# Two attention layers on one core: row position terms from PSUM, one transfer per query block, and half of the division on ScalarE

## The chip, the cores and the metric

The kernel runs on one core of one Trainium2 chip. The metric is the device time in microseconds. A core has a matrix engine (PE, TensorE), a vector engine (DVE, VectorE), an activation engine (ACT, ScalarE), a general engine (POOL, GpSimd) and a sequencer that only issues transfers (SP, SyncE). Each works through its own instructions in order and waits on semaphores. PE writes into PSUM, which DVE and ACT can read; the other data lie in SBUF or in DRAM.

## What is computed

Two layers, each `x = x + attention(group_norm(x))`, on an input of 4 images of 32 x 32 positions (S = 1024) with 768 channels, in float32. There are 12 heads of 64 channels. For one image and one head:

```python
q, k, v  = split(group_norm(x) @ Wqkv)          # layer 1 has biases too
rel_h    = einsum('hwc,hkc->hwk', q, Rh)         # Rh[h,k] = rel_pos_h[h - k + 31]
rel_w    = einsum('hwc,wkc->hwk', q, Rw)         # Rw[w,k] = rel_pos_w[w - k + 31]
scores   = scale * q @ k.T + rel_h[..., :, None] + rel_w[..., None, :]
out      = softmax(scores) @ v
x        = x + concat_heads(out) @ Wproj + bproj
```

The position terms depend on the query and on the key's row (rel_h) or column (rel_w) alone. Layer 1 clips its tables at 14 positions and scales differently; the shape of the work is the same.

## The kernel before

Layers and images are taken one after another: 8 "images" (layer, image), each with 6 pairs of heads, 48 pairs g in all. The two heads of a pair lie in the lower and upper 64 of 128 partitions. A pair is cut into 8 blocks n of 128 queries, four image rows each. The loop over units (g, n) at the end of `attention_blocks` writes the order out by hand. In unit (g, n) it emits, for every engine in this order: what is due in the list `early`; the biases of the unit after next (POOL); the scores of the next unit (PE), with their reduction (DVE) and exponential (ACT); the reads due from `behind`; the transposes of this unit (`turn`, DVE); the division of the next unit (`divide`); then a share of other products from the list `todo`, by `take`; and, after blocks 2 and 6, `weigh`, the product of weights and values. So the tight loop of a unit runs scores, reduction, exponential, reciprocal, division, transpose, write to DRAM, read back, weigh, spread over several units.

The other products are the projections of the next pair (`project_in` for q and k, `project_values` for v) and the output products (`project_out`). They are cut into chunks, and `shares` says how many chunks a unit takes. `later` and `early` are lists of small steps: what is put in `later` in a unit runs at the start of the unit after next or, if a step of `early` puts it there, of the next one.

Position terms: `positions` multiplies a half of q (4 blocks) by both tables, 128 columns a head, of which the first 64 are for the row and the last 64 for the column. ACT copies the whole result from PSUM into t (L286) and sends it to DRAM (tdr, L288). `diagonals` then reads both kinds of terms back with shifted strides into rel, 16 transfers of 32 KB a pair (L307). The row term of a query needs 32 of 63 table entries, and the start of the 32 depends on the image row only, which is the same for 32 neighbouring partitions.

Transposing the weights: `turn` transposes 32 x 32 squares on DVE (L370) into tb. A tile tb holds two blocks of one head; after the second block both heads' tiles are written to DRAM (td, L373), 1 MB each, and queued in `behind` or `behind2`. `read_back` (L381) reads a tile into pt with keys in the partitions. `weigh` (L399) multiplies one or two quarters (two blocks each) by the values of both heads, and DVE evicts the sum (L408 in layer 0, L411 with a bias in layer 1).

Buffers that matter: two PSUM tiles `ps_s` for scores, and two PSUM tiles `ps_m` that projections, position terms, weigh and output products take in turns, so that a product can start only when the product before last has been evicted. The projections are evicted by ACT and then DVE (L227 or L229, then L230; L259, then L260).

Queues: SP issues nearly all transfers in order, and waits in that order. ACT issues tdr; in the first pair it also issues half of rel, and at the very end the last reads of pt.

At the end, the last pair has no projections ahead of it. Its `todo` holds the rest of the last image's output products in three parts (`cuts`): channels 0 to 2, channels 3 and 4, and channel 5, which is the last pair itself. Its first 30 chunks run in the units, 12 after them, then two weighs and the last six products.

Of the kernel before, what the change touches and what calls it, by code (L numbers as in the profile page):

```python
# [31 lines left out]
FP = mybir.dt.float32  # L32
AF = mybir.ActivationFunctionType
ALU = mybir.AluOpType
ENGINES = {getattr(mybir.EngineType, e) for e in ("PE", "DVE", "Activation", "Pool", "SP")}

P = 128
B, HW, C = 4, 32, 768
S = HW * HW
NH, D = 12, 64  # L40
NC = C // P
NT = S // P
# [5 lines left out]
NP = NH // 2  # L48
# [6 lines left out]
def attention_blocks(ctx: ExitStack, tc: tile.TileContext, a: dict, out: bass.AP):  # L55
    nc = tc.nc
# [7 lines left out]
    qkpool = ctx.enter_context(tc.tile_pool(name="qk", bufs=2))  # L64
    vpool = ctx.enter_context(tc.tile_pool(name="v", bufs=3))
    scpool = ctx.enter_context(tc.tile_pool(name="sc", bufs=6))
    tmppool = ctx.enter_context(tc.tile_pool(name="tmp", bufs=1))
    tbpool = ctx.enter_context(tc.tile_pool(name="tb", bufs=3))
    ptpool = ctx.enter_context(tc.tile_pool(name="pt", bufs=2))
    relpool = ctx.enter_context(tc.tile_pool(name="rel", bufs=2))  # L70
    iopool = ctx.enter_context(tc.tile_pool(name="io", bufs=4))
    small = ctx.enter_context(tc.tile_pool(name="small", bufs=4))
    dram = ctx.enter_context(tc.tile_pool(name="scratch", bufs=1, space=bass.MemoryType.DRAM))
    dram2 = ctx.enter_context(tc.tile_pool(name="scratch2", bufs=2, space=bass.MemoryType.DRAM))
    ps_s = ctx.enter_context(tc.tile_pool(name="ps_s", bufs=2, space=PSUM))
    ps_m = ctx.enter_context(tc.tile_pool(name="ps_m", bufs=2, space=PSUM))
# [2 lines left out]
    mid = [dram.tile([C, S], FP, tag=f"mid{b}", name=f"mid{b}") for b in range(B)]  # L79
# [4 lines left out]
    NPAIR = NI * NP  # L84
# [33 lines left out]
    for l in range(LAYERS):  # L118
        tab = const.tile([P, 2, 2 * HW], FP, tag=f"tab{l}", name=f"tab{l}")
        nc.gpsimd.memset(tab, 0.0)  # L120
        for i, ax in enumerate("hw"):
            src = a[f"rel{ax}{l}"]
            n = src.shape[1]
# [10 lines left out]
    for l in range(LAYERS):  # L134
        t = const.tile([P, NC], FP, tag=f"bo{l}", name=f"bo{l}")
        nc.sync.dma_start(out=t, in_=a[f"bo{l}"])
        bo.append(t)
    bqkv = const.tile([P, 3, NP], FP, tag="bqkv", name="bqkv")
# [130 lines left out]
    def positions(g, i):  # L269

        l = images[g // NP][0]
        q = qk_of[g, 0]
        if i == 0:
            t_of[g] = dram2.tile([S, 2 * P], FP, tag="tdr", name=f"tdr_{g}")
            rel_of[g] = relpool.tile([P, 2, 2, NT, HW], FP, tag="rel", name=f"rel_{g}")
        ps = ps_m.tile([P, 2, 4, P], FP, tag="m", name=f"tp_{g}_{i}")
        for j in range(4):
            for h in range(2):
                rows = slice(h * D, (h + 1) * D)
                at = 4 * i + j  # L280
                nc.tensor.matmul(  # L281
                    ps[:, h, j, :], lhsT=q[rows, at * P : (at + 1) * P], rhs=tabs[l][rows, :],
                    start=True, stop=True,
                )
        t = tmppool.tile([P, 4, 2, P], FP, tag="tmp", name=f"t_{g}_{i}")
        nc.scalar.copy(t, ps.rearrange("p h j r -> p j h r"))  # L286
        td = t_of[g]
        nc.scalar.dma_start(  # L288
            out=td[i * HALF : (i + 1) * HALF, :].rearrange("(j p) r -> p j r", p=P),
            in_=t.rearrange("p j h r -> p j (h r)"),  # L290
        )
        if i == 1:
            later.append(lambda: diagonals(g))

    def diagonals(g):
        td = t_of[g]
        for h in range(2):
            for ax in range(2):
                for y in range(4):


                    at = HW * y * 2 * P + h * P + HW - 1 + 2 * HW * ax - (y if ax == 0 else 0)
                    src = bass.AP(
                        td.tensor, td.offset + at,
                        [[2 * P - ax, HW], [P * 2 * P - (4 if ax == 0 else 0), NT], [1, HW]],
                    )
                    (nc.scalar if h and not g else nc.sync).dma_start(out=rel_of[g][32 * y : 32 * y + 32, h, ax, :, :], in_=src)  # L307


    sc_of, st_of, tb_of, pt_of, attn_of = {}, {}, {}, {}, {}  # L310
# [39 lines left out]

    def divide(g, n):
        st = st_of[g, n]
        nc.vector.reciprocal(st[:, 2, :], st[:, 1, :])  # L353
        for h in range(2):
            sc = sc_of[g, n, h].rearrange("p k j -> p (k j)")
            nc.gpsimd.tensor_scalar(sc, sc, st[:, 2, h : h + 1], 1.0, ALU.mult, ALU.mult)  # L356

    def turn(g, n):

        quarter, j = divmod(n, 2)
        for h in range(2):
            if j == 0:
                tb_of[h] = tbpool.tile([P, HW, 2, HW], FP, tag="tb", name=f"tb_{g}_{n}_{h}")
            tb = tb_of[h]
            nc.vector.transpose(tb[:, :, j, :], sc_of[g, n, h])  # L370
            if j == 1:
                td = dram2.tile([P, S * 2], FP, tag=f"td{h}", name=f"td_{g}_{n}_{h}")
                nc.sync.dma_start(out=td, in_=tb.rearrange("p k n i -> p (k n i)"))  # L373
                (behind if quarter % 2 else behind2).append(
                    lambda queue=None, h=h, td=td: read_back(g, quarter, h, td, queue)
                )

    def read_back(g, quarter, h, td, queue=None):
        pt = ptpool.tile([P, 4, NT, 2 * HW], FP, tag=f"pt{h}", name=f"pt_{g}_{quarter}_{h}")
        pt_of[g, quarter, h] = pt  # L380
        (queue or nc.sync).dma_start(  # L381
            out=pt.rearrange("p r k t -> p r (k t)"),
            in_=td.rearrange("(r j) (a t) -> (j a) r t", r=4, a=4),
        )

    def weigh(g, quarters):

        if quarters[0] == 0:
            attn_of[g] = apool.tile([P, S], FP, tag="attn", name=f"attn_{g}")
        n = len(quarters)
        av = ps_m.tile([P, S], FP, tag="m", name=f"av_{g}_{quarters[0]}")[:, : n * 2 * P]
        for at, quarter in enumerate(quarters):
            for k in range(NT):
                for h in range(2):
                    rows = slice(h * D, (h + 1) * D)
                    nc.tensor.matmul(  # L399
                        av[rows, at * 2 * P : (at + 1) * 2 * P], lhsT=v_of[g][:, k, rows],  # L400
                        rhs=pt_of[g, quarter, h][:, :, k, :], start=(k == 0), stop=(k == NT - 1),
                    )
        at = quarters[0] * 2 * P
        to = attn_of[g][:, at : at + n * 2 * P].rearrange("p (q n r i) -> p q r n i", q=n, n=2, r=4)
        av = av.rearrange("p (q r n i) -> p q r n i", q=n, n=2, r=4)
        im, pair = divmod(g, NP)
        if images[im][0] == 0:
            nc.vector.tensor_copy(to, av)  # L408
        else:
            for q in range(n):  # L410
                nc.vector.tensor_scalar(to[:, q], av[:, q], bqkv[:, 2, pair : pair + 1], None, ALU.add)  # L411

    def cuts(im):
        return [0, NC // 2, NC] if im + 1 < NI else [0, NC // 2, NC - 1, NC]
# [86 lines left out]

    early, mid, later, behind, behind2 = [], [], [], [], []

    def run(todo):
        while todo:  # L510
            todo.pop(0)()
# [12 lines left out]
    def take(groups, n):  # L524

        while groups and n > 0:
            group, count = groups[0]
            if next(group, None) is None:
                groups.pop(0)
            else:  # L530
                groups[0] = (group, count - 1)
                n -= 1
        while groups and groups[0][1] == 0:
            for _ in groups.pop(0)[0]:
                pass
# [6 lines left out]
    with tc.manual_schedule(engines=ENGINES):  # L542
# [8 lines left out]
        todo = prepare(0)  # L551
# [14 lines left out]
        for at, (g, n) in enumerate(units):  # L566
            im, pair = divmod(g, NP)
            end = im + 1 == NI
            if n == 0:
                shares = [6, 6, 0, 6, 12, 6, 0, 12]  # L570
                ins = (todo if at == 0 else []) + prepare(g + 1)
                if pair < 3:
                    if at == 0:
                        shares = [12, 6, 0, 6, 12, 6, 0, 0]
                    todo = ins + (put_out(im - 1, 1, range(4 * pair, 4 * pair + 4)) if im else [])
                elif pair < NP - 1:
                    todo = ins + put_out(im, 0, range(4 * pair - 12, 4 * pair - 8))
                    if pair == 3 and not end:
                        stages, apply = norm(im + 1)
                else:  # L580
                    todo = ins + put_out(im, 0, range(8, 12))
                    if end:
                        fetch_last()
                        todo += put_out(im, 1, range(12)) + put_out(im, 2, range(0, 12, 2))
                        shares = [6, 6, 0, 6, 6, 2, 0, 4]
            if (pair, n) in loads and not end:
                load_x(im + 1, loads[pair, n])
            if im + 1 < B:
# [9 lines left out]
                biases(*units[at + 2])  # L598
            if at + 1 < len(units):
                scores(*units[at + 1])  # L600
            run(behind)
            behind, behind2 = behind2, behind
            if pair == 3 and n in stages and not end:
                stages[n]()
            if pair == 4 and n in (2, 4, 6) and not end:
                apply(n // 2 - 1)
            share = shares[n]
            first = 3 if n == NT - 1 else 2 if end and pair == NP - 1 and n in (3, 4) else 0
            first = min(first, share)
            take(todo, first)  # L610
            share -= first
# [11 lines left out]
                weigh(g, (0, 1))  # L623
            elif n == 2 and g:
                weigh(g - 1, (2, 3))
        for read in behind:
            read(nc.scalar)
        take(todo, 12)
        for quarter in (2, 3):
            weigh(NPAIR - 1, (quarter,))  # L630
        todo = put_out(NI - 1, 2, range(1, 12, 2))
# [56 lines left out]
```

## Time and profile before

| | us |
|---|---|
| median of 3 runs (3507.12 to 3509.28) | 3508.29 |
| the profiled execution's span | 3507.0 |
| median less that span | 1.3 |
| PE busy | 3462.3 (99%) |
| POOL busy | 2729.9 (78%) |
| DVE busy | 2381.1 (68%) |
| ACT busy | 1227.5 (35%) |
| weight loads of PE, beside its products | 1921.4 (55%) |
| DMA, mean rate over the span | 309 GB/s |

The profile is of one execution. Busy time is what an engine spent in instructions; a group of instructions is named by line, engine, operation and "written<-read" tiles, with the count and the mean duration. A wait is the idle time of an engine before an instruction, put down to what released it. The chain of waits follows the work that ended last back to the start. Most matrix products work in two halves of PE side by side, so their durations add up to more than PE's busy time. The profile counts two records for one float32 matmul. Granted clock is the share of PE's full clock. Transfers in DRAM and back are named by the tile written and the tile read, and can be followed from issue to landing.

### The profile page before, as it was taken

The numbers are of one execution on the slowest core, as the hardware profiler recorded it, in microseconds if no ns is written. First come the engines' busy times: TensorE is split into PE (matmuls) and PEld (weight loads), VectorE is DVE, ScalarE is ACT, GpSimd is POOL, SyncE is SP. The second block draws the span as 40 slices with busy tenths as digits, with TensorE's granted clock in tenths as the row PEclk, the third lists the DMA queues.
The fourth block names the chain that finished last, engine by engine and source line by source line (L and its number), as shares of the span: only waits on it lengthen the run. The fifth ranks groups of instructions, "written<-read, shape, count | busy, mean of one in ns | idle before, by whom it ended". The sixth has DMA issues, their size and how long they took to land.

```text
span 3507.0 us, 55102 instructions
## 1 busy us (share of the span) xinstructions
PE 3462.3 (99%) x21120; PEld 1921.4 (55%) x21120; DVE 2381.1 (68%) x3676; ACT 1227.5 (35%) x2040; POOL 2729.9 (78%) x1546
## 2 busy tenths in 40 slices
PE   6999999999999999999999999999999999999999
PEld 4555555555555555555555555555555555555554
DVE  4666767767677676767767667666666667666666
ACT  2334333333333333333333333333333333333331
POOL 3888887778777787788777788787787778787774
PEclk9999999999999999999999999999999999999999
DMA  4889989999899898898989989899889988898877
GB/s 137 312 308 311 332 293 337 319 316 326 304 329 323 313 316 313 312 324 305 326 305 326 320 292 332 311 331 306 300 327 324 321 298 316 319 322 295 311 275 281
DMA packets 624857, 1084.54 MB, mean 309 GB/s; under 512 B 247120, under 2 KB 310096, under 8 KB 575440
## 3 DMA queue, kind: packets, MB, share of 16 engines
q1 hardware_dynamic: 569008, 1028.29, 83.4%
q10 hardware_dynamic: 55584, 52.72, 4.4%
q8 instruction: 166, 2.72, 0.3%
q14 instruction: 99, 0.81, 0.1%
HBM read 580.59 MB, written 500.27 MB: 308 GB/s over the span
## 4 chain that ended last, share of the span: by engine, by line
PE 97%; DMA 2%; DVE 0%; SPq 0%; issue 0%; ACT 0%; POOL 0%; ACTq 0%; DVEq 0%
PE pj L214 28%; PE s L333 19%; PE av L399 19%; PE o L475 14%; PE pv L249 14%; PE tp L281 3%; DMA tdr<-t 1%; DMA pt<-td 1%; SPq L307 0%; DMA td<-tb 0%; DMA wo<-in_wo 0%; DMA xn<-in_x 0%; DVE st L152 0%; DMA rel<-tdr 0%; DMA per<-mv 0%
## 5 line engine op out<-in xcount | busy, mean ns | idle before, releaser
L319 POOL TENSOR_TENSOR sc<-rel 128x1024 f32<-128x1024 f32 x768 | 1890.4, 2485 | 38.2 <-DMA rel<-tdr 38.2
L356 POOL TENSOR_SCALAR sc<-sc,sm 128x1024 f32<-128x1024 f32 x768 | 855.1, 1127 | 686.1 <-DVE sm L353 669.2
L346 ACT ACTIVATE sc<-sc,sm 128x1024 f32<-128x1024 f32 x768 | 879.8, 1147 | 1370.9 <-DVE sm L342 1368.7
L342 DVE CUSTOM_DVE_ANT_0 sc<-s,sc 128x1024 f32<-128x1024 f32 x768 | 909.8, 1222 | 293.3 <-PE s L333 266.4
L214 PE MATMUL pj<-xn,w 64*128 64x512 f32 x4608 | 1033.5, 591 | 26.8 <-DVE xn L193 25.7
L370 DVE STREAM_TRANSPOSE tb<-sc 128x1024 f32<-128x1024 f32 x768 | 910.7, 1222 | 22.9 <-DMA td<-tb 20.5
L214 PEld LDWEIGHTS pj<-xn,w 64*128 64x128 f32 x4608 | 453.2, 188 | 568.6 <-issue 536.6
L333 PE MATMUL s<-k,q 64*128 64x512 f32 x3072 | 750.1, 598 | 7.0 <-DVE sm L342 6.9
L399 PE MATMUL av<-pt,v 128*64 128x256 f32 x6144 | 689.1, 382 | 6.1 <-DMA pt<-td 6.1
L399 PEld LDWEIGHTS av<-pt,v 128*64 128x64 f32 x6144 | 434.5, 137 | 289.8 <-ACT v L259 35.6
L249 PE MATMUL pv<-wv,xn 64*128 64x256 f32 x4608 | 515.7, 376 | 0.0
L249 PEld LDWEIGHTS pv<-wv,xn 64*128 64x128 f32 x4608 | 448.3, 187 | 90.8 <-issue 30.1
L475 PE MATMUL o<-attn,wo 128*128 128x512 f32 x1080 | 475.8, 597 | 0.2 <-DMA wo<-in_wo 0.2
L333 PEld LDWEIGHTS s<-k,q 64*128 64x128 f32 x3072 | 288.5, 187 | 299.5 <-issue 275.5
L475 PEld LDWEIGHTS o<-attn,wo 128*128 128x128 f32 x1080 | 201.4, 190 | 271.4 <-issue 260.9
L260 DVE TENSOR_TENSOR v<-pv,v 128x256 f32<-128x256 f32 x192 | 81.5, 425 | 277.6 <-ACT v L259 277.6
L259 ACT COPY v<-pv 128x256 f32<-128x256 f32 x192 | 71.5, 372 | 330.7 <-PE pv L249 282.9
L286 ACT COPY t<-tp 128x1024 f32<-128x1024 f32 x96 | 97.2, 1012 | 245.5 <-PE tp L281 148.5
L346 ACT ACTIVATION_READ_ACCUMULATOR sc<-sc,sm 128x1 f32 x768 | 143.6, 187 | 0.0
L230 DVE TENSOR_TENSOR q<-pj,q 128x512 f32<-128x512 f32 x96 | 66.4, 692 | 107.5 <-ACT q L227 56.0
L230 DVE TENSOR_TENSOR k<-pj,k 128x512 f32<-128x512 f32 x96 | 66.4, 692 | 95.5 <-ACT k L227 49.0
L281 PEld LDWEIGHTS tp<-tab,q 64*128 64x128 f32 x1536 | 100.0, 187 | 39.9 <-issue 39.6
(34 smaller groups left out, 787.6 us busy)
## 6 DMA issues: line engine op xcount, KB each, us to landing
td<-tb SPq DMA_DIRECT2D x384, 1024.0 KB, 5.9
pt<-td SPq DMA_DIRECT2D x382, 1024.0 KB, 7.6
tdr<-t ACTq DMA_DIRECT2D x96, 512.0 KB, 6.3
w<-in_wqk SPq DMA_DIRECT2D x96, 384.0 KB, 7.5
rel<-tdr SPq DMA_DIRECT2D x760, 32.0 KB, 2.3
part<-res SPq DMA_DIRECT2D x84, 256.0 KB, 5.5
res<-part SPq DMA_DIRECT2D x84, 256.0 KB, 9.1
wv<-in_wv SPq DMA_DIRECT2D x24, 768.0 KB, 8.7
```

The costliest lines, as they stand in the source:

```text
L214: nc.tensor.matmul(t[:, a, :], lhsT=w[rows, c, :], rhs=xn[c][rows, cols], start=(c == 0), stop=(c == NC - 1),)
L230: nc.vector.tensor_tensor(to, t[1], to, ALU.add)
L249: nc.tensor.matmul(t[:, a, k, :], lhsT=xn[c][rows, (2 * i + k) * P : (2 * i + k + 1) * P], rhs=w[rows, c, :], start=(c == 0), stop=(c == N ...
L281: nc.tensor.matmul(ps[:, h, j, :], lhsT=q[rows, at * P : (at + 1) * P], rhs=tabs[l][rows, :], start=True, stop=True,)
L319: nc.gpsimd.tensor_tensor(sc.rearrange("p (a k) (u l) -> p a (k u) l", a=4, l=8), rel[:, h, 0, n, :].unsqueeze(1).unsqueeze(3).to_broadcas ...
L333: nc.tensor.matmul(ps[h][:, cols], lhsT=q[rows, n * P : (n + 1) * P], rhs=k[rows, cols], start=True, stop=True,)
L342: nc.vector.tensor_tensor_reduce(out=sc, in0=ps[h], in1=sc, scale=-scale, scalar=BIG, op0=ALU.add, op1=ALU.min, accum_out=st[:, 0, h : h + 1],
L346: nc.scalar.activation(sc, sc, AF.Exp, bias=st[:, 0, h : h + 1], scale=-1.0, accum_out=st[:, 1, h : h + 1],)
L356: nc.gpsimd.tensor_scalar(sc, sc, st[:, 2, h : h + 1], 1.0, ALU.mult, ALU.mult)
L370: nc.vector.transpose(tb[:, :, j, :], sc_of[g, n, h])
L399: nc.tensor.matmul(av[rows, at * 2 * P : (at + 1) * 2 * P], lhsT=v_of[g][:, k, rows], rhs=pt_of[g, quarter, h][:, :, k, :], start=(k == 0) ...
L475: nc.tensor.matmul(t, lhsT=wo_of[im, o, c], rhs=attn_of[im * NP + c][:, cols], start=(c == c0), stop=(c == c1 - 1),)
```

## The change

Six things are changed.

1. Row terms: after the table product, ACT copies only the column half (64 of 128 columns) into t, and sends that to DRAM. Then ACT copies the row terms straight from PSUM into rel, four copies of 32 partitions per half. `diagonals` reads back the column terms alone, 8 transfers a pair. t has two buffers instead of one.
2. A tile tb holds one block of both heads. It is written in one transfer of 1 MB, once per block, and read back in one transfer of 1 MB; pt holds two blocks of both heads. tb has two buffers instead of three, td five instead of two per head. The list `behind` becomes four lists in rotation. The reads fall in the same units as before.
3. The second head is divided by ACT instead of POOL; in the last pair both heads are.
4. The sums of `weigh` are evicted by ACT instead of DVE, in one instruction.
5. In the last pair the units take 18 chunks instead of 30, and 24 instead of 12 follow after the last unit; the last unit takes none ahead of its transposes.
6. The builder reserves 1024 bytes a partition of scratch memory for transfers instead of its default.

```diff
-    tmppool = ctx.enter_context(tc.tile_pool(name="tmp", bufs=1))
-    tbpool = ctx.enter_context(tc.tile_pool(name="tb", bufs=3))
+    tmppool = ctx.enter_context(tc.tile_pool(name="tmp", bufs=2))
+    tbpool = ctx.enter_context(tc.tile_pool(name="tb", bufs=2))
...
+    dram4 = ctx.enter_context(tc.tile_pool(name="scratch4", bufs=5, space=bass.MemoryType.DRAM))
...
-        t = tmppool.tile([P, 4, 2, P], FP, tag="tmp", name=f"t_{g}_{i}")
-        nc.scalar.copy(t, ps.rearrange("p h j r -> p j h r"))
+        t = tmppool.tile([P, 4, 2, 2 * HW], FP, tag="tmp", name=f"t_{g}_{i}")
+        nc.scalar.copy(t, ps[:, :, :, 2 * HW :].rearrange("p h j r -> p j h r"))
...
+        for y in range(4):
+            rows = slice(y * HW, (y + 1) * HW)
+            at = ps[rows, :, 0, HW - 1 - 4 * 4 * i - y : 2 * HW - 1 - 4 * 4 * i - y]
+            src = bass.AP(at.tensor, at.offset, [at.ap[0], at.ap[1], [P - 4, 4], [1, HW]])
+            nc.scalar.copy(rel_of[g][rows, :, 0, 4 * i : 4 * i + 4, :], src)
...
     def diagonals(g):
         td = t_of[g]
         for h in range(2):
-            for ax in range(2):
-                for y in range(4):
...
+            for y in range(4):
+                src = bass.AP(
+                    td.tensor, td.offset + HW * y * P + h * 2 * HW + HW - 1,
+                    [[P - 1, HW], [P * P, NT], [1, HW]],
+                )
+                (nc.scalar if h and not g else nc.sync).dma_start(
+                    out=rel_of[g][y * HW : (y + 1) * HW, h, 1, :, :], in_=src
+                )
...
     def divide(g, n):
         st = st_of[g, n]
+        last = g + 1 == NPAIR
...
-            nc.gpsimd.tensor_scalar(sc, sc, st[:, 2, h : h + 1], 1.0, ALU.mult, ALU.mult)
+            if h == 0 and not last:
+                nc.gpsimd.tensor_scalar(sc, sc, st[:, 2, h : h + 1], 1.0, ALU.mult, ALU.mult)
+            else:
+                nc.scalar.mul(sc, sc, st[:, 2, h : h + 1])
 
     def turn(g, n):
...
+        tb = tbpool.tile([P, HW, 2, HW], FP, tag="tb", name=f"tb_{g}_{n}")
         for h in range(2):
...
+            nc.vector.transpose(tb[:, :, h, :], sc_of[g, n, h])
+        td = dram4.tile([P, S * 2], FP, tag="td", name=f"td_{g}_{n}")
+        nc.sync.dma_start(out=td, in_=tb.rearrange("p k h i -> p (k h i)"))
+        behind[(2, 1, 1, 0)[n % 4]].append(lambda queue=None: read_back(g, n, td, queue))
+
+    def read_back(g, n, td, queue=None):
+        quarter, u = divmod(n, 2)
+        if u == 0:
+            pt_of[g, quarter] = ptpool.tile(
+                [P, 2, 4, NT, 2, HW], FP, tag="pt", name=f"pt_{g}_{quarter}"
+            )
         (queue or nc.sync).dma_start(
-            out=pt.rearrange("p r k t -> p r (k t)"),
+            out=pt_of[g, quarter][:, u].rearrange("p r k h i -> p r (k h i)"),
...
-                        rhs=pt_of[g, quarter, h][:, :, k, :], start=(k == 0), stop=(k == NT - 1),
+                        rhs=pt_of[g, quarter].rearrange("p n r k h i -> p (n r) k h i")[:, :, k, h, :],
+                        start=(k == 0), stop=(k == NT - 1),
...
-            nc.vector.tensor_copy(to, av)
+            nc.scalar.copy(to, av)
         else:
-            for q in range(n):
-                nc.vector.tensor_scalar(to[:, q], av[:, q], bqkv[:, 2, pair : pair + 1], None, ALU.add)
+            nc.scalar.activation(to, av, AF.Identity, bias=bqkv[:, 2, pair : pair + 1])
...
-                        shares = [6, 6, 0, 6, 6, 2, 0, 4]
+                        shares = [3, 3, 0, 3, 3, 2, 0, 4]
...
-            run(behind)
-            behind, behind2 = behind2, behind
+            run(behind[0])
+            behind.append(behind.pop(0))
...
-            first = 3 if n == NT - 1 else 2 if end and pair == NP - 1 and n in (3, 4) else 0
+            first = 0 if at + 1 == len(units) else 3 if n == NT - 1 else 2 if end and pair == NP - 1 and n in (3, 4) else 0
...
-        for read in behind:
-            read(nc.scalar)
-        take(todo, 12)
+        for reads in behind:
+            for read in reads:
+                read(nc.scalar)
+        take(todo, 24)
...
-    nc = bacc.Bacc("TRN2", target_bir_lowering=False, num_devices=1)
+    nc = bacc.Bacc("TRN2", target_bir_lowering=False, num_devices=1, dynamic_dma_scratch_size=1024)
```

## The prediction

> **What bounds the kernel now.** I read the waits of TensorE first, then busy time by stage, then the timeline where a wait stood. The page gives PE 3462.3 us of a span of 3507.0. All that PE waited for, longest first (total us, times, longest):
>
> ```profile
> PE pj L214 <- DVE xn L193: 25.7, 1, 25.7
> PE s L333 <- DVE sm L342: 6.9, 6, 1.4
> PE av L399 <- DMA pt<-td: 6.1, 3, 3.0
> ```
>
> The first is the start, before anything is normalized; the change leaves it. Between 206 and 3410 us there is a single wait, of 1.4 us: the middle is PE end to end. Stages of one pair of heads each, and the last pair (length; busy time of PE, PEld, DVE, ACT, POOL; granted clock; DMA share; GB/s):
>
> ```profile
> 1000.00:1071.69 71.69, 71.69 (x444) 39.80 (x442) 51.97 (x83) 24.93 (x43) 56.59 (x33) 1.00 0.89 317
> 2000.00:2071.69 71.69, 71.69 (x442) 39.81 (x440) 47.95 (x80) 27.98 (x46) 56.50 (x33) 1.00 0.88 313
> 3418.10:3503.90 85.80, 81.64 (x345) 36.49 (x344) 57.01 (x86) 16.64 (x28) 42.41 (x26) 0.98 0.80 284
> ```
>
> A pair takes 71.69 us, all PE; work taken from POOL, DVE or DMA there buys nothing. Time can be won only where PE stood: first pair and last pair. The first pair, chain of work (start, us, what), then PE's timeline:
>
> ```profile
> 92.17 12.20 DMA tdr<-t
> ...
> 113.77 8.84 DMA pt<-td
> ```
> ```profile
> 119.04 0.65 PE L399 MATMUL av<-pt,v 128*64 128x256 f32 x2 [0.74 <-DMA pt<-td]
> 122.66 5.35 PE L399 MATMUL av<-pt,v 128*64 128x256 f32 x30 [2.98 <-DMA pt<-td]
> 127.94 1.99 PE L333 MATMUL s<-k,q 64*128 64x512 f32 x8
> ```
>
> The position transfer tdr landed at 104.4; SP, which issues in order, stood behind it, then issued 16 rel transfers (8.8 us), and only then the reads of pt that weigh needs. The last pair, the chain again:
>
> ```profile
> 3472.64 2.29 DVE tb L370 x2
> 3474.95 6.29 DMA td<-tb
> ...
> 3481.33 10.04 DMA pt<-td
> ```
>
> From the last transpose to the last pt 16.4 us pass in DMA, more than PE had work left to cover.
>
> **What the Trainium skill says.** "TensorE: Matmul & The Clock Gate", Part 1: an idle window of some 3.4 us halves PE's clock. The trace agrees: after the 2.4 us wait near 3491 the granted clock is 0.59, and it is 0.79 at 120 to 125 us. A wait costs more than its length. "ScalarE: Activation LUTs", section on table sets: copies and identities are in every set; the trace agrees, its 16 table loads stand at L181 and L346 alone, so the new multiplies and copies load none. "SBUF — State Buffer", Door 1: runs of at least a 16-byte line read at full rate; weigh's new runs are 128 bytes, and no run here shows it.
>
> **The change, part by part.**
>
> *Position terms.* Per half: the copy t is 512 elements a partition, not 1024: 586 ns (row of L227) for 1012. Four row copies of 256 elements, priced by L259's 372 ns, come behind t's DMA issue. ACT gains 384 x 0.372 - 96 x 0.426 = 102 us. tdr goes from 512 to 256 KB, 96 times; rel reads from 768 to 384, 32 KB each. On SP a pair issues 8 fewer, about 0.5 us each with gaps: 4.4 us.
>
> First pair, start: t's copy ends 0.43 earlier (47.15), the transfer, 2.91 for twice the size, I take as 2.5; 4 issues per queue instead of 8 save 2.1 us of the 4.2 on SP. POOL's first bias starts at 54.0, not 56.73. PE's second scores then wait only for their predecessors' two DVE reductions (1.15 each behind scores ending 59.3): they end near 63.2 instead of 64.4. Gain 1.2 us, at most 2.4 (the two waits), at least 0.
>
> First pair, weigh: with two tmp buffers ACT no longer waits for the first tdr. The second tdr is issued near 89.8, not 92.2: the multiply queued ahead of it holds it to there. Even if it lands as slowly (12.2), SP is free at 102, issues 8 rel in 4.4 us, reads at about 106.5, landing 8.8 later at 115.5; quarter 1 of weigh needs it at about 117. Both waits go. Between the scores at 112.06 and those at 127.94 lie 15.88 us; work is 1.92 + 7.06 (scores, weigh): 6.9 over what gap-free work takes, of which I count 6.5. That is 3.7 of waits and the rest half-clock. Ends: 0 to 8.
>
> *One tile and transfer per block.* Same MB, same 2 KB pieces: td is written 1 MB every block instead of 2 MB every second; reads fall in the same blocks (3, 4, 7, 0). The extra issue slots lie in SP's waits: SP waits 1117.6 us for transposes. DVE's 20.5 us of waiting for td goes, behind PE. The moving operand of weigh is 8 runs of 32 elements for 4 of 64. I take 0. The bounds: av takes 7.06/32 = 220.6 ns per two-matmul slot, pv with one contiguous run 215.8; if all 4.8 came from 3 more runs, 4 further cost 6.4 ns x 3072 = 20 us. Against: o with one run has 437.5 where pj has 429, so the excess follows the way weights are loaded.
>
> *Second head divided on ACT.* 392 multiplies (last pair: both heads). The trace has none; the skill's ScalarE page (What ACT_TABLE_LOAD costs) gives 186 + 93 for a pointer operand + 0.833 x 1024 = 1132 ns, 93 of it overlapped; exp on the same tile is 1147 here, starting the next after 1.05. I take 1.04 in line; ends 1.0 to 1.25. POOL loses 392 x 1.127 = 442 us, all slack. ACT: 1227 + 444 + 102 + 61 (below) = 1834, 52%: no bound. But the multiply adds a wait: it stands behind DVE's reciprocal, and queued behind it are the q, k and v evictions. For them wait DVE's add, and for that PE's PSUM buffer. The tight place, once a pair, is block 1 to 2, second layer:
>
> ```profile
> 2062.60 0.12 DVE L353 RECIPROCAL sm<-sm 128x2 f32<-128x2 f32 x1
> ...
> 2063.09 0.69 ACT L229 ACTIVATE q<-pj,bqkv 128x512 f32<-128x512 f32 x1 [1.37 <-PE pj L214]
> ...
> 2069.48 0.13 DVE L353 RECIPROCAL sm<-sm 128x2 f32<-128x2 f32 x1
> ...
> 2069.96 0.69 ACT L229 ACTIVATE q<-pj,bqkv 128x512 f32<-128x512 f32 x1 [1.35 <-PE pj L214]
> ...
> 2070.68 0.69 DVE L230 TENSOR_TENSOR q<-pj,q 128x512 f32<-128x512 f32 x1 [1.07 <-ACT q L229]
> ...
> 2072.45 0.87 PE L399 MATMUL av<-pt,v 128*64 128x256 f32 x6
> ```
>
> The add ends 2071.37; weigh takes that buffer at 2072.45: slack 1.08. New: the first eviction starts at 2062.72 + 0.03 + 1.04 = 2063.79, 0.70 late; DVE had 0.40 + 0.08 free before its next reduction, so the second reciprocal is 0.22 late; its eviction starts at 2069.61 + 0.22 + 1.07 = 2070.90, 0.94 late. Slack left 0.14, less 0.05 for the signal. No stall; with 1.25 twice in line 0.33 per pair, x 24 = 8 us (first layer, eviction 0.1 shorter and slack 1.18: half that). I charge 1 us in all.
>
> *Weigh evicted on ACT.* DVE loses 75 us; ACT gains 48 x 0.586 + 49 x 0.688 = 61. After the second weigh, the buffer's next user comes behind tp and scores, 2.8 us later: hidden, at 0.7.
>
> *Last pair.* 12 chunks of product (two matmul records, 0.875 us each) leave the blocks for the end: 24 there, 21 us. Blocks then hold 1.92 + 2.63 of PE and run at DVE's pace: reductions 2.3, transposes 2.3, reciprocal 0.12, eviction 0.66 = 5.4 instead of 7.26. PE's sum from 3418.1 is 7 scores x 1.92, 42 chunks 36.75, three weighs 21.2, six last chunks 5.25: 76.6, where the last product ended 85.0 later. By my walk through the blocks PE stands 0.3 + 0.5 + 1.4 + 0.5 us and 0.6 at the last eviction, 3.3 in all; transposes end near 3462.8, the 1 MB write lands by 3469, the read by 3477, while PE has chunks until 3485. Gain 85.0 - 79.9 = 5.1; ends 1 and 8.4.
>
> *Smaller scratch* in the builder: no work.
>
> Sum on the profiled execution: 3507.0 - 1.2 - 6.5 - 5.1 + 1 = 3495.2. The median, 3508.3, lies 1.3 above the profiled span; with it 3496.5, 11.8 faster (0.34%). About 0.2%, 7 us, is what a measurement of this kernel can tell from no change.
>
> **Rivals.**
> *A part is not won (0.20).* The pt wait only moves (a tdr as slow as before plus slower pt reads), or the clock falls at the three places with no product (131, 197, 262 us: one costs 1.7), or the tail keeps its wait: two of the three gains halved, about 3503, no difference. For: DMA is at 0.97 to 1.05 there. Against: the margin above.
> *Weigh reads slower (0.06).* 20 us as worked out: 3516. It passes no change from 6.2 ns per slot on.
> *The multiply stalls the middle (0.08), the one that ends slower.* In block 1 to 2 evictions wait for the multiply. Each 0.1 us beyond the slack is 4.8 us over 48 pairs; gains are eaten at 0.27, and it is slower by 0.2% from 0.4 us on. At 0.6: 3508.3 - 12.8 + 28.8 = 3524. For: slack falls from 1.08 to 0.1. Against: it needs a multiply of some 1.5 us, above exp's 1.15.
>
> **How the numbers follow.** Forecast 3496.5, chance 0.66; its own range 3490 to 3501.3. The range 3489 to 3512 takes in the first rival and half of weigh's bound, and leaves out the slow ends. Faster by over 0.2%: 0.66 and a little of the first rival, 0.68. Within: 0.19. Slower: 0.13.
>
> **What would show it.** PE's waits for pt gone at 119 and at the end; rel issues 384 on SP and ACT; a pair still 71.69 us; ACT near 1830, POOL near 2290, DVE near 2300; PE busy, without a wait, from the last pair's first end chunk to the last weigh. Wrong if a pair is longer than 71.69 (then see whether weigh's slot grew over 220.6, or PE waits for DVE's q at block 2), or if the last weigh waits for pt.

## The result, and the profile after

The changed kernel took 3514.6 us (median of 20, 3509.8 to 3516.8) where the kernel before took 3508.7 (median of 20, 3506.4 to 3514.5): ratio 1.0014, 95% interval 1.0007 to 1.0020. No time was saved; 5.9 us were lost, within the 0.2% that count as no change. The forecast of 3496.5 was 18 us too low, and the time lies above the range given. The profiled execution spans 3511.3 us against 3507.0.

What PE waited for in it, longest first (us in total, times, longest):

```profile
PE pj L215 <- DVE xn L194: 25.9, 1, 25.9
PE av L399 <- DVE q L231: 7.7, 7, 1.2
PE s L337 <- DVE sm L346: 6.4, 6, 1.4
PE o L471 <- ACT attn L410: 2.8, 2, 2.2
PE av L399 <- DMA pt<-td: 2.4, 2, 1.3
```

Before, `av` waited for pt three times, 6.1 us; that is 2.4 now. But seven waits of `av` for q are new, and so is one for an eviction on ACT. The stages answering to those of before (length; busy time of PE, PEld, DVE, ACT, POOL; granted clock; DMA share; GB/s):

```profile
1000.00:1071.69 71.69, 71.69 (x444) 39.83 (x442) 50.32 (x80) 36.80 (x60) 47.73 (x25) 1.00 0.88 306
2000.00:2071.69 71.69, 71.69 (x442) 39.85 (x440) 45.68 (x77) 40.12 (x64) 47.80 (x25) 1.00 0.88 303
3419.13:3507.28 88.15, 82.74 (x345) 36.48 (x344) 54.15 (x79) 33.38 (x46) 24.56 (x10) 0.98 0.78 271
```

An ordinary pair is as long as before and has no wait: the moved work costs it nothing. The last pair is 3.1 us longer, not 5.1 shorter. The first pair, PE's timeline (start, us, instruction, wait ahead of it):

```profile
113.39 7.13 PE L399 MATMUL av<-pt,v 128*64 128x256 f32 x64
120.45 1.99 PE L337 MATMUL s<-k,q 64*128 64x512 f32 x8
```

The 64 records of weigh run in one piece at full clock; before, two waits cut them. The scores behind start at 120.45 instead of 127.94.

Where the time went follows from the starts of the same instructions in both traces. The table sets them out for all kernels run; the experiments are told below. The first three columns are the time won (-) or lost against the profiled execution of before: where the weigh in block 2 of the second pair starts, where that in block 6 of the fourth pair does, and where that in block 6 of the 47th does, the last pair but one. "Last pair" runs from its first scores to the end of the last matmul. The ratio is of times, with its 95% interval.

```
                        2nd pair  4th pair  47th pair  last pair   span    ratio to before
before                     0         0         0        85.0     3507.0
changed                  -9.2      -7.2      +1.0       88.2     3511.3   1.0014 (1.0007..1.0020)
e5  changed, again       -6.1      -6.0      +2.2       85.6     3509.9   1.0016 (1.0010..1.0023)
e1  tb x3                -6.3      -5.9      +2.3       82.3     3506.7   1.0001 (0.9992..1.0009)
e2  one POOL division    -6.2      -3.8      -3.8       85.1     3503.5   0.9991 (0.9983..0.9999)
e3  multiply late        -7.0      -5.4      -5.4       86.4     3503.1   0.9989 (0.9982..0.9995)
e4  old end              -6.0      -5.9      +2.3       86.5     3510.7   1.0009 (1.0001..1.0017)
e6  e1 and e3            -7.6      -7.3      -7.3       81.1     3496.0   0.9977 (0.9970..0.9984)
e7  e6, old end          -6.1      -4.2      -4.2       86.7     3504.5   0.9992 (0.9984..1.0000)
e8  before, positions    -7.2      -5.5      -5.5       83.1     3499.6   0.9979 (0.9972..0.9987)
e9  before, divide       +4.2      +5.9     +14.3       82.7     3519.0   1.0023 (1.0013..1.0033)
```

The row of the changed kernel reads: 9.2 us won in the first pairs, 2.0 given back by the fourth (1.7 of it by a low clock, as told below), 8.2 lost by the 47th (7.7 of them are the seven waits themselves), 3.1 in the last pair. With 0.2 behind the last matmul, that is the 4.3 by which the spans differ. The loads themselves came out as forecast: ACT is busy for 1810.3 us, POOL for 2290.3, DVE for 2306.5.

**The seven waits.** They stand at one place, block 2 of the last pair of each image but the last. In the pair before, VectorE normalizes the next image's inputs (`apply`). The last of the seven, before, on VectorE:

```profile
2983.96 2.73 DVE L193 TENSOR_SCALAR xn<-xn,nrm 128x1024 f32<-128x1024 f32 x2
...
2987.26 2.26 DVE L193 TENSOR_SCALAR xn<-xn,nrm 128x1024 f32<-128x1024 f32 x1
...
2990.11 1.21 DVE L342 CUSTOM_DVE_ANT_0 sc<-s,sc 128x1024 f32<-128x1024 f32 x1
...
2995.84 0.69 DVE L230 TENSOR_TENSOR q<-pj,q 128x512 f32<-128x512 f32 x1 [1.04 <-ACT q L229]
2996.93 1.22 DVE L342 CUSTOM_DVE_ANT_0 sc<-s,sc 128x1024 f32<-128x1024 f32 x1 [0.40 <-PE s L333]
...
3002.71 0.69 DVE L230 TENSOR_TENSOR q<-pj,q 128x512 f32<-128x512 f32 x1 [1.07 <-ACT q L229]
3004.68 1.23 DVE L342 CUSTOM_DVE_ANT_0 sc<-s,sc 128x1024 f32<-128x1024 f32 x1 [1.28 <-PE s L333]
```

And after:

```profile
2983.74 4.02 DVE L194 TENSOR_SCALAR xn<-xn,nrm 128x1024 f32<-128x1024 f32 x2
...
2988.34 2.26 DVE L194 TENSOR_SCALAR xn<-xn,nrm 128x1024 f32<-128x1024 f32 x1
...
2991.19 1.21 DVE L346 CUSTOM_DVE_ANT_0 sc<-s,sc 128x1024 f32<-128x1024 f32 x1
...
2997.67 0.69 DVE L231 TENSOR_TENSOR q<-pj,q 128x512 f32<-128x512 f32 x1 [1.79 <-ACT q L230]
2998.27 1.22 DVE L346 CUSTOM_DVE_ANT_0 sc<-s,sc 128x1024 f32<-128x1024 f32 x1
...
3004.76 0.69 DVE L231 TENSOR_TENSOR q<-pj,q 128x512 f32<-128x512 f32 x1 [1.79 <-ACT q L230]
3005.37 1.22 DVE L346 CUSTOM_DVE_ANT_0 sc<-s,sc 128x1024 f32<-128x1024 f32 x1
```

Two things differ. Two normalizations take 4.02 us for 2.73 (the first 1.20 in both, the second 2.90 for 1.60), so block 0 of the next pair is reduced 1.1 us later, though PE started its scores 0.2 us earlier (2987.71 for 2987.94). Then VectorE waits 1.79 us per block for q's eviction, where it waited 1.05, because ScalarE's multiply stands ahead of it. A block costs VectorE 7.1 us in this way. Before, VectorE came out ahead and waited for scores (0.40, 1.28); now it never does, and carries the lateness to the add of q that weigh waits for:

```profile
3005.51 0.87 PE L399 MATMUL av<-pt,v 128*64 128x256 f32 x6 [1.18 <-DVE q L231]
```

Why is the normalization longer? POOL's side of the same stretch, before and then after:

```profile
2983.50 2.65 POOL L356 TENSOR_SCALAR sc<-sc,sm 128x1024 f32<-128x1024 f32 x2 [2.22 <-DVE sm L353]
2986.11 5.75 POOL L319 TENSOR_TENSOR sc<-rel 128x1024 f32<-128x1024 f32 x2
```
```profile
2983.27 1.12 POOL L362 TENSOR_SCALAR sc<-sc,sm 128x1024 f32<-128x1024 f32 x1 [1.96 <-DVE sm L358]
2984.35 5.70 POOL L323 TENSOR_TENSOR sc<-rel 128x1024 f32<-128x1024 f32 x2
```

A normalization takes 0.81 us while POOL does nothing (the six at the kernel's start). All 42 others start in the course of a POOL instruction and end 0.55 to 0.56 us after it does, in both kernels. Before, the second ended at 2986.69, the second division at 2986.14; after, at 2987.76, the first bias add at 2987.21. The division that left POOL took 1.55 us there; the add that moved up into its place takes 2.86. The Trainium skill ("SBUF — State Buffer", Who interferes with whom) says that a two-port VectorE instruction such as tensor_scalar and a GpSimd instruction exclude each other, and that the one issued first keeps the shared ports to its end. These times agree, for the instruction in whose course the normalization starts.

**The last pair.** VectorE's waits for a free tb buffer, and ScalarE behind them, after:

```profile
3438.09 2.37 DVE L370 STREAM_TRANSPOSE tb<-sc 128x1024 f32<-128x1024 f32 x2 [3.94 <-DMA td<-tb]
...
3463.72 2.37 DVE L370 STREAM_TRANSPOSE tb<-sc 128x1024 f32<-128x1024 f32 x2 [3.72 <-DMA td<-tb]
```
```profile
3466.17 2.19 ACT L364 ACTIVATE sc<-sc,sm 128x1024 f32<-128x1024 f32 x2 [4.56 <-DVE sm L358]
3468.26 0.67 ACT L410 ACTIVATE attn<-av,bqkv 128x512 f32<-128x512 f32 x1
```

The chain of work (start, us, what) shows what the second of these waited for:

```profile
3446.02 8.59 DMA td<-tb
3454.61 0.02 issue
3454.62 0.36 SPq L381
3454.99 0.04 issue
3455.03 8.59 DMA td<-tb
```

SP issues in order. Its read of pt waits for the td written at 3446.02; the next td's write stands behind that read and goes out only at 3455.03. Until it has landed, the buffer that the transposes want is not free. The reciprocal, the two multiplies and then weigh's eviction queue behind those transposes, and the products behind the eviction. PE waits 2.19 us, and its clock falls with it (the window's last numbers are granted clock, DMA share and GB/s):

```profile
3468.98 24.86 PE L471 MATMUL o<-attn,w_last 128*128 128x512 f32 x52 [2.19 <-ACT attn L410]
```
```profile
3464.90:3480.00 15.10, 12.91 (x26) 5.47 (x27) 7.39 (x11) 2.76 (x3) 0.00 (x0) 0.89 0.88 299
```

### The profile page after: what moved, and what is told of

Read it like the earlier page. It is cut to its first block, busy times and chain, and to the rows that moved or that the text cites. A ratio compares the mean times of both kernels' runs of the same rounds, so it can differ in the third digit from the quotient of the medians.

```text
span 3511.3 us, 55069 instructions
## 1 busy us (share of the span) xinstructions
PE 3460.9 (99%) x21120; PEld 1920.0 (55%) x21120; DVE 2306.5 (66%) x3532; ACT 1810.3 (52%) x2913; POOL 2290.3 (65%) x1154
## 4 chain that ended last, share of the span: by engine, by line
PE 94%; DVE 2%; DMA 2%; issue 1%; ACT 0%; SPq 0%; DVEq 0%; ACTq 0%
PE pj L215 26%; PE av L399 19%; PE s L337 19%; PE pv L250 14%; PE o L471 14%; PE tp L282 2%; DMA td<-tb 1%; DVE tb L370 1%; DVE sc L346 1%; DMA pt<-td 0%; DVE st L153 0%; DVE q L231 0%; DVE res L482 0%; DMA per<-mv 0%; ACT q L230 0%
## 5 line engine op out<-in xcount | busy, mean ns | idle before, releaser
L350 ACT ACTIVATE sc<-sc,sm 128x1024 f32<-128x1024 f32 x768 | 880.3, 1147 | 792.1 <-DVE sm L346 790.6
L362 POOL TENSOR_SCALAR sc<-sc,sm 128x1024 f32<-128x1024 f32 x376 | 420.3, 1118 | 1099.5 <-DVE sm L358 1069.0
L370 DVE STREAM_TRANSPOSE tb<-sc 128x1024 f32<-128x1024 f32 x768 | 907.9, 1220 | 14.6 <-DMA td<-tb 12.9
L364 ACT ACTIVATE sc<-sc,sm 128x1024 f32<-128x1024 f32 x392 | 449.2, 1148 | 499.6 <-DVE sm L358 499.6
L297 ACT COPY rel<-tp 32x256 f32<-32x256 f32 x384 | 139.4, 363 | 53.9 <-ACT t L287 27.8
```

The lines of the kernel that those rows point to most:

```text
L297: nc.scalar.copy(rel_of[g][rows, :, 0, 4 * i : 4 * i + 4, :], src)
L350: nc.scalar.activation(sc, sc, AF.Exp, bias=st[:, 0, h : h + 1], scale=-1.0, accum_out=st[:, 1, h : h + 1],)
L364: nc.scalar.mul(sc, sc, st[:, 2, h : h + 1])
L370: nc.vector.transpose(tb[:, :, h, :], sc_of[g, n, h])
```

## The experiments

The theory was that two separate losses ate the gain: the border waits, which need both a slower normalization and the multiply ahead of q's eviction, and the tb buffers in the last pair. The rivals: one of the two causes alone, weigh's eviction on ScalarE, SP's queue whatever the buffers, or the late products themselves.

**e1, three tb buffers.**

```
-    tbpool = ctx.enter_context(tc.tile_pool(name="tb", bufs=2))
+    tbpool = ctx.enter_context(tc.tile_pool(name="tb", bufs=3))
```

> The changed kernel with three tb buffers instead of two. Theory (last pair: the transposes wait for a tb buffer because SP issues the td write late, and everything behind them on DVE and ACT is late with them): the two waits of DVE for tb (3.94 and 3.72 us) are gone, PE's wait for the eviction of weigh (2.19 us) with them, and the last pair, from its first scores to the last sum, shrinks by 2 to 4 us of 88; the span falls from 3511.3 to 3507.5 to 3509.5. Rival (SP's queue is the cause, and a third buffer only lets the transposes run ahead of writes that are issued no sooner): DVE's waits go but pt lands as late, and the span stays within 1 us of 3511.3. The seven waits of PE for q (7.7 us) stay under both.

3508.2 us, ratio 1.0001 where the changed kernel has 1.0016 (e5). The last pair takes 82.3 us, 3.3 and 5.9 less than in the changed kernel's two profiles (e5 is the second); the span, 3506.7, fell 0.8 us further than the expected range. PE's waits from 3390 us on:

```profile
PE av L399 <- DMA pt<-td: 0.9, 1, 0.9
PE o L471 <- ACT attn L410: 0.6, 1, 0.6
PE s L337 <- DVE sm L346: 0.2, 1, 0.2
```

VectorE no longer waits for tb in the last pair, and PE's wait of 2.2 us for ScalarE has gone with it, though the order of SP's queue and weigh's eviction on ScalarE are as they were. So the rival is refuted: the third buffer alone takes this loss away. The seven waits stand (7.8 us).

**e2, one division back on POOL.**

```
-            if h == 0 and not last:
+            if (h == 0 and not last) or (g % NP, n) == (NP - 1, 0):
```

> The changed kernel, with POOL dividing the second head of one query block in 48 as before: block 0 of an image's last pair, whose division stands beside the normalization on DVE. Theory (PE's wait of 1.2 us at seven image borders needs both causes: a normalization that runs 1.3 us longer because POOL's bias add runs beside it, and the multiply ahead of q's eviction that lets DVE recover nothing): the pair of normalizations takes 2.7 us again instead of 4.0, all seven waits go, the span falls by 7 to 8.5 us, to about 3503. Rival 1 (the multiply alone is the cause): blocks 1 and 2 still have it, the waits stay, span within 1 us of 3511.3. Rival 2 (the eviction of weigh on ScalarE is the cause): the waits stay too.

3505.3 us, ratio 0.9991. All seven waits are gone: the table shows no change between the fourth and the 47th pair. One of an image's 48 blocks decides 8.2 us. Its stretch on VectorE:

```profile
2980.19 2.72 DVE L194 TENSOR_SCALAR xn<-xn,nrm 128x1024 f32<-128x1024 f32 x2
...
2986.34 1.21 DVE L346 CUSTOM_DVE_ANT_0 sc<-s,sc 128x1024 f32<-128x1024 f32 x1
...
2999.92 0.69 DVE L231 TENSOR_TENSOR q<-pj,q 128x512 f32<-128x512 f32 x1 [1.79 <-ACT q L230]
3000.91 1.23 DVE L346 CUSTOM_DVE_ANT_0 sc<-s,sc 128x1024 f32<-128x1024 f32 x1 [0.30 <-PE s L337]
```

The multiply still makes VectorE wait 1.79 us in blocks 1 and 2; without the late start that is not enough to stall PE. Rivals 1 and 2 are refuted: with weigh's eviction and the multiplies of blocks 1 and 2 in place there is no wait at the borders.

**e3, the multiply behind its block's products.** The second head's `nc.scalar.mul` is taken out of `divide` into a function `second`, in all pairs but the last:

```
             take(todo, share)
+            if at + 1 < len(units) and units[at + 1][0] + 1 < NPAIR:
+                second(*units[at + 1])
             if n == 6:
```

> The changed kernel with ScalarE's multiply of the second head put behind the products of its block, and so behind q's, k's and v's evictions, in all pairs but the last. Theory (both causes are needed): the normalization still takes 4.0 us for two, the reduction of the last pair's block 0 still starts 3.5 us after its scores, but DVE's wait for q's eviction falls from 1.79 to about 1.05 us per block and it catches up before weigh: the seven waits go, the span falls by 7 to 8.5 us to about 3503. Rival 1 (the slow normalization alone is the cause): the waits fall by less than half, the span by less than 4 us. Rival 3 (the multiply, late now, holds up the next transposes): new waits of PE in all pairs, the span above 3511.3.

3503.8 us, ratio 0.9989. The normalization is as slow as in the changed kernel (4.04 us for two), and still no wait for q is left:

```profile
2978.52 4.04 DVE L194 TENSOR_SCALAR xn<-xn,nrm 128x1024 f32<-128x1024 f32 x2
...
2990.60 0.66 DVE L231 TENSOR_TENSOR q<-pj,q 128x512 f32<-128x512 f32 x1
2991.47 1.23 DVE L346 CUSTOM_DVE_ANT_0 sc<-s,sc 128x1024 f32<-128x1024 f32 x1 [0.21 <-issue]
...
2997.27 0.69 DVE L231 TENSOR_TENSOR q<-pj,q 128x512 f32<-128x512 f32 x1 [1.08 <-ACT q L230]
2999.23 1.23 DVE L346 CUSTOM_DVE_ANT_0 sc<-s,sc 128x1024 f32<-128x1024 f32 x1 [1.28 <-PE s L337]
```

With the eviction ahead of the multiply VectorE catches up within two blocks. e2 and e3 each take away one cause and keep the other; each removes all of the loss at the borders. Both causes are needed.

In both, one wait stands in the fourth pair, ahead of the stretch compared here: PE waits for weigh's eviction, 1.9 us at 286 in e2 and 1.2 us at 284 in e3. Just before, VectorE waited 5.6 and 4.7 us for a tb buffer, and the multiply and the eviction queued behind its transposes as in the last pair. With three tb buffers (e1, e6) that wait is not there.

**e4, the products of the last pair given out as before.**

```
-                        shares = [3, 3, 0, 3, 3, 2, 0, 4]
+                        shares = [6, 6, 0, 6, 6, 2, 0, 4]
...
-            first = 0 if at + 1 == len(units) else 3 if n == NT - 1 else 2 if end and pair == NP - 1 and n in (3, 4) else 0
+            first = 3 if n == NT - 1 else 2 if end and pair == NP - 1 and n in (3, 4) else 0
...
-        take(todo, 24)
+        take(todo, 12)
```

> The changed kernel with the last pair's products given out as before (6, 6, 0, 6, 6, 2, 0, 4 and 12 at the end, three of them ahead of the last transpose). Theory (the late products help at the very end, but with 12 fewer in the blocks PE reaches the waits in the middle of the pair sooner): PE waits less before 3470 and more after the last transposes, where pt is awaited; the wait for the last pt is at least 3 us again, the last pair within 2 us of the 88 that it takes now, 3509 to 3513. Rival (the late products are the cause of the loss in the last pair): the last pair takes 85 us or less as before the change, the span falls by 3 us or more, to 3508 or less.

3510.5 us, ratio 1.0009. PE waits 3.8 us ahead of the last weigh and not in the middle; the last pair takes 86.5 us, between the 85.6 and 88.2 of the changed kernel's two profiles. So with two tb buffers the late products win nothing clear, and the rival, which asked for 85 us or less, is refuted: they alone did not lengthen the pair. VectorE has no wait for tb in this last pair, though it has two buffers: the blocks take 7.3 us each, not 5.3. The waits for tb in the last pair come of the two buffers and the shorter blocks together. The wait for the last pt, 3.8 us here and in e7, is 2.4, 2.1 and 1.8 in the three kernels that keep the old tiles (before, e8, e9); what makes it longer was not tested.

**e5, the changed kernel again**, beside e6 to e8 on one chip.

> The changed kernel as it is, beside the next three on one chip. Theory: the seven waits of PE for q (7.7 us) and a last pair of 88 us come back, span 3510 to 3512, 0.1% above the kernel before. Rival (the loss is a matter of one profiled execution): the waits or the length of the last pair differ by more than 2 us.

3513.0 us, 1.0016; the seven waits are 7.7 us again. The last pair is 85.6 us this time, 2.6 shorter than in the first profile: the rival's bound of 2 us is passed for that size. Of the 2.6, 1.7 is the clock: PE waits 2.19 us for the same eviction, but the 52 records behind it take 23.16 us here and 24.86 in the first profile. VectorE's waits for tb are much the same, 7.5 us for 7.7.

**e6, both repairs: e1's buffers and e3's multiply.**

> The changed kernel with both repairs: ScalarE's multiply behind its block's products, and three tb buffers. Theory (the two losses are separate, one at the image borders, one in the last pair): they add up. Against the kernel before, 5 us gained by the first images and held to the last pair, which takes 82 us for 85: span 3498 to 3500, 0.2% under the kernel before. Rival (with no borders' waits the last pair meets its transfers sooner, and gives back what the first repair won): last pair 85 us or more, span 3502 or more.

3498.5 us, ratio 0.9977 (0.9970 to 0.9984), faster than both kernels. The profiled span, 3496.0, is 2 us below the range expected. The last pair takes 81.1 us; from 200 us to the last pair PE waits once, 1.8 us. The repairs add, within the noise of the ratios: e1 is 0.0015 and e3 0.0027 below e5, e6 is 0.0039 below it.

**e7, e6 with the products given out as before** (e4's edit).

> As e6, but with the last pair's products given out as before the change. Theory (with three tb buffers the late products are worth what stands between the last transposes and the last pt): PE waits 3 to 5 us for the last pt, the last pair takes 85 to 87 us, the span is 3 to 5 us above that of e6. Rival (the tb buffers made the whole of it, and the late products give nothing): last pair within 1 us of that of e6.

3503.9 us, ratio 0.9992, 5.4 us above e6. The last pair takes 86.7 us, for 81.1. PE at its end, e7:

```profile
3480.46 3.67 PE L404 MATMUL av<-pt,v 128*64 128x256 f32 x32
3487.95 6.34 PE L404 MATMUL av<-pt,v 128*64 128x256 f32 x32 [3.81 <-issue]
```

The last quarter stands 3.8 us, then runs at a lower clock (6.34 us for 3.67). In e6 the same two quarters run in one piece:

```profile
3478.44 7.13 PE L404 MATMUL av<-pt,v 128*64 128x256 f32 x64
```

So the late products are worth 5.4 to 5.6 us with three tb buffers, a little more than the 3 to 5 expected, and nothing clear with two (e4). With the old end, in turn, the third buffer is worth nothing: the last pair takes 86.7 us with it and 86.5 without.

**e8, the kernel before with the position terms alone.** `positions` and `diagonals` are those of the changed kernel, and tmp has two buffers.

> The kernel before with the part on position terms alone (row terms copied from PSUM by ScalarE, half as large a transfer, two tmp buffers). Theory: PE's two waits for pt in the first pair (3.7 us) and the low clock behind them go, 6 to 7.5 us by the first pair's second weigh; no waits at the image borders, since nothing stands ahead of q's evictions and POOL still divides both heads; last pair 85 us as before. Span 3499.5 to 3502. Rival 1 (the gain of the first pair needs the smaller transfers of the other part as well): less than 3 us gained there. Rival 2 (ScalarE's row copies, not the multiply, make q's evictions late): waits at the image borders, span above 3505.

3500.2 us, ratio 0.9979 (0.9972 to 0.9987). This part alone wins 7.2 us by the second pair and 5.5 by the fourth. No wait stands at the borders, so ScalarE's row copies don't cause them: both rivals are refuted. The last pair takes 83.1 us, not the 85 expected, and 82.7 in e9, which hands out its products in the same way. The 85.0 of the kernel before holds 1.7 us of low clock: the 30 records behind its wait for pt take 5.35 us, in e8 and e9 3.67.

**e9, the kernel before with the second head divided by ScalarE alone.**

```
-            nc.gpsimd.tensor_scalar(sc, sc, st[:, 2, h : h + 1], 1.0, ALU.mult, ALU.mult)
+            if h == 0 or g + 1 == NPAIR:
+                nc.gpsimd.tensor_scalar(sc, sc, st[:, 2, h : h + 1], 1.0, ALU.mult, ALU.mult)
+            else:
+                nc.scalar.mul(sc, sc, st[:, 2, h : h + 1])
```

> The kernel before with the second head divided by ScalarE alone, in all pairs but the last; everything else as before (position terms whole through memory, weigh evicted by VectorE). Theory (this part alone makes the border loss, by both of its sides: POOL's next bias add stands beside the normalization sooner, and the multiply stands ahead of q's eviction): seven waits of PE for q of 1.0 to 1.3 us, 7 to 9 us, span 3514 to 3516, 0.2% slower; the last pair takes 85 us. Rival (ScalarE's other new work, row copies and weigh's evictions, is needed for the waits too): fewer than seven waits or under 4 us of them, span below 3511.

3516.2 us, ratio 1.0023 (1.0013 to 1.0033). The borders cost 8.4 us (14.3 less 5.9) as in the changed kernel, so this part makes them by itself, and the rival is refuted. Not expected was a loss of 5.9 us in the first pairs, with PE waiting for ScalarE's copy of t (1.4) and for q (2.7) there. I take it that ScalarE, now with more to do, falls behind where the whole position terms still wait for their transfer; this was not tested further. No run has the change of tiles and transfers (part 2) or the smaller scratch memory (part 6) alone.

## Why the prediction was wrong

The parts that it priced as gains exist: e6, with two repairs, takes 3498.5 us where 3496.5 was forecast. The prediction failed on two steps that it had priced at nearly nothing: the multiply at the image borders (1 us said, 8.2 measured), and the tb buffers in the last pair (left out of its walk; a gain of 5.1 became a loss).

**First scores, -1.2.** POOL's first bias add starts at 52.7 (54.0 was said), and the second wait of the scores goes, the first stays, as said. First weigh starts 1.23 earlier; but 0.76 of that is luck: the first 48 projection records, ahead of anything changed, took 12.17 us in that execution for 13.06, and the last projection of the start begins at 46.27 for 47.03. From there to first weigh pass 67.12 us, before 67.59. So 0.47 belongs to the change (0.45 in e1): over-sized.

**First pair's weigh, -6.5.** Right: both waits went. Between first weigh and the next one 8.0 us were won in this profile, e7 and e8, and 6.3 in e1 to e6. The 1.7 between them is the clock behind the next wait of the scores, in these seven records and those that follow. It was low before and in e1 to e6, full here (before, then after):

```profile
131.36 3.45 PE L333 MATMUL s<-k,q 64*128 64x512 f32 x7 [1.43 <-DVE sm L342]
```
```profile
123.86 2.70 PE L337 MATMUL s<-k,q 64*128 64x512 f32 x7 [1.43 <-DVE sm L346]
```

That is luck too, and it was given back: behind the third wait of this kind the clock stayed full before (seven records in 2.70 us at 262.39) and fell after (4.07 us at 253.23). The rival had named these places and their price.

**Tile and transfer per block, 0.** The rival on weigh's reads is refuted: 64 records in 7.13 us, 4 runs or 8. But "DVE's 20.5 us of waiting for td goes, behind PE" failed. 12.9 us of such waits remain, and 7.7 of them are in the last pair, where they reach PE.

**Multiply on ScalarE, +1.** Its price was right: 1148 ns each, the next instruction 1.06 us later. The slack at block 1 to 2 of an ordinary pair held: 71.69 us, and no wait for q outside the borders. The step that failed is "The tight place, once a pair": the walk was made on one pair inside an image and carried over to all. It let VectorE begin the block on time. At the seven borders VectorE now begins block 0 1.1 us late out of the normalization, and with the multiply ahead of each eviction of q it has no free time left to catch up; there it cost 8.2 us, not 1. VectorE was late because POOL's next bias add moved up beside the normalization and held it: the 442 us that POOL lost, put down as "all slack", were slack for POOL but not for VectorE. The rival that ends slower had the mechanism right (evictions behind the multiply) and the place wrong, and it asked for a slower multiply where a late VectorE was enough.

**Weigh evicted on ScalarE.** 585 and 677 ns; in the changed kernel no wait in the middle, as said (e2 and e3 have one each). In the last pair its eviction stood behind two multiplies (2.19 us), through the tb buffers, and PE waited 2.19 us for it; with three buffers 0.6 is left.

**Last pair, -5.1.** Measured +3.1 (88.15), where both profiles hold 1.7 us of low clock; e5 (85.6) and e8 (83.1, products given out as before the change) hold none of it, and differ by 2.5. The 5.4 us per block, VectorE's pace, is right where no buffer is missing: from transposes to transposes, 3443.62 to 3448.89, pass 5.3 us. What failed is the walk, which left out the buffers of tb. Before, three buffers held two blocks of a head each, three blocks' worth; after, two hold one block each, and a write stands in SP's queue behind a read and then takes 8.6 us to land. The walk had the last transposes end 44.7 us behind the pair's first scores (3462.8 less 3418.1). They end at 50.6, and with three buffers at 46.0 (e1) and 44.9 (e6). With three buffers the pair takes 82.3 and 81.1 us (79.9 said).

**From span to median, +1.3.** It is 3.3 after the change, another 2 us, and this says nothing of the kernel: every run's time stands 1.7 to 1.9 us above its own span, and the changed kernel's profiled execution (3513.1) was 1.5 shorter than its median.

The sum by these steps, on the two profiled executions: 3507.0, less 7.2 (first pairs, luck and low clock included), plus 8.2 (borders), 3.1 (last pair) and 0.2: 3511.3.

## What to carry to other kernels

Look for the tight place in the stages that differ, not in the common one: a wait that stayed hidden in the ordinary pairs cost 8 us at the seven where the engine behind it was already late, and putting the new instruction behind the evictions that others wait for made it free. When an engine is relieved, ask what it will now do sooner and which engine that stands beside. When the layout of a buffer changes, count how many steps of work its buffers hold, not the buffers, and how long a step will take once other work is moved out of it; and look for the read ahead of its write in an in-order queue.

## What the runs showed of the hardware

A normalization that starts in the course of a POOL instruction ended 0.55 us after it, to within about 0.01 us, in 42 of 42 cases in each of the two kernels, whether POOL's instruction took 1.12, 1.55, 2.5 or 2.86 us; it lasted from 0.85 to 2.92 us where it takes 0.81 alone. What VectorE's time came to was set by where in POOL's instruction it started, not by its own work.

PE's clock fell after short waits. Each profile has three places in the first pairs where PE waits 1.43 to 1.80 us for VectorE and has no other product to run (131, 197 and 262 us in the kernel before). Behind some of them matmuls take 1.06 us for 0.59, which costs 1.7 us, and behind others of the same length they don't: at two of the three in ten of the eleven profiles, at one in e9, and not at the same ones. The prediction took its trace to agree with an idle window of 3.4 us; its own trace had the low clock behind waits of 1.43 and 2.4 us. Which of these waits is followed by it stays open. It is part of why the profiles differ in the table's first column.
